# Attention and a depthwise convolution: a new order of work, and four steps moved to other engines

## The chip, the cores and the metric

The kernel runs on one core of one Trainium2 chip. It uses the core's engines side by side: TensorE (PE) for matrix products, VectorE (DVE), ScalarE (ACT) and GpSimd (POOL) for elementwise work, and SyncE (SP) for issuing transfers. POOL issues transfers too. Each engine takes its instructions from its own queue in order, and waits on semaphores for what other engines or transfers bring. The metric is the device time of one execution in microseconds (us); less is better. All data is float32.

## The reference

The input x has 16 images of 384 channels and 32 x 32 points. Two layers are computed, each with a group normalisation ahead (32 groups of 12 channels) and its input added behind:

```python
x = x + _L0_conv_ref(_gn(x), L0_conv_w_qkv, L0_conv_w_proj, L0_conv_b_proj)
x = x + _L1_conv_ref(_gn(x), L1_conv_weight)

# layer 0: attention over the 1024 points of an image, 8 heads of 48 channels
qkv = einsum('bnc,oc->bno', xt, w_qkv)
attn = softmax(einsum('bhnd,bhmd->bhnm', q, k) * SCALE)
out = einsum('bnc,oc->bno', einsum('bhnm,bhmd->bhnd', attn, v), w_proj) + b_proj

# layer 1: depthwise 7 x 7 convolution, padding 3, with a symmetrised weight
w_sym = (weight + rot90(weight, 1) + rot90(weight, 2) + rot90(weight, 3)) * 0.25
```

## The kernel before

**Tiles.** An image is three tiles of 128 channels by 1024 points. Heads go in pairs: four pairs per image, numbered `u` over the whole run (64 in all). `wqk` has its columns arranged so that three products give q and k of pairs 0 to 2 in full and one third of pair 3 each; `qk_rest` gathers pair 3 with six small transfers on POOL's queue.

**One image, or batch `b`.** `load_x` brings x to `xns[b]` on POOL's queue (one buffer: the next image can come only after the last use by `v_step`). `Stats.channels` takes per-channel statistics on DVE (`bn_stats`, L180). `exchange` (L184 to L195) spreads each group's twelve channels to all its rows by way of DRAM: three transfers on SP's queue. `groups` (L197 to L204) merges them on all 128 rows, three times 144 values, and raises the variance to the power -1/2 on POOL. `apply` (L206) normalises on DVE. Then come ten pieces on PE, called chunks: six `qk_step` (L216; 12 matmuls, copied out by ACT) and four `v_step` (L244; 12 matmuls, copied out by ACT).

**Attention.** A pair takes 16 steps (two halves of the queries, eight key tiles), so a batch takes 64 and the run 1024. `s_step` (L268) computes scores in PSUM (three buffers) and ACT takes the exponential to a tile `e`; `av_step` (L284) multiplies with v, which carries a column of ones, so the sums of the softmax come with it. `take` (L298) copies the result to `os_[u]`. `sums_out`, `invert` and `divide` (L304 to L334) send the sums through DRAM, take reciprocals on DVE, spread these over 64 rows each by way of DRAM, and multiply on DVE; for the last pair of a batch, six transfers on SP's queue put its rows to the other pairs.

**Projection and convolution.** `proj_step` (L338) computes a tile of the projection, and ACT adds the bias into a tile `y`. The old x was loaded again by `load_rest` (L138, POOL's queue), and `residual` (L352) adds `y` on DVE, giving x1. Statistics, exchange and merging follow as for x. `conv_begin` (L359) normalises x1 to `xn1s` on DVE, and 49 `conv_tap` (L363) on DVE each multiply a shifted window of it by one weight per channel and add it to x1 in place; `conv_end` (L375) stores the tile by POOL's queue. The very last tile is convolved on PE instead (`conv_on_pe` makes diagonal matrices on ACT, `conv_on_pe_run` multiplies, L380 to L415).

**The order.** The program is unrolled in Python by a planner (L497 to L698). It keeps two clocks, `clock` for PE and `vclock` for DVE, and adds fixed costs for each piece of work (L497). PE's part is a loop over groups of `GS` = 3 steps; in each turn the scores of a group are emitted and then the value steps of the group before, and where `credit` allows, one chunk of the next batch or one projection. `catch_up` (L526) then emits DVE's work until `vclock` has reached `clock`: first what is due in `later` (statistics, inversions and so on, entered by `after` with a delay and a cost), else a tap. Up to two tiles are open for taps, in turn. A batch's taps can start only when its x1 is there, so they are done during the next batch's attention. The framework beneath sets the semaphores, and puts the instructions of each engine in a queue; that order is near to the program's, and not always the same.

Of the kernel before, what the change touches and what calls it, by code (L numbers as in the profile page):

```python
# [16 lines left out]
P = 128  # L17
# [23 lines left out]
def kernel(  # L41
# [59 lines left out]
    def run(general):  # L101
        tag = "g" if general else "f"
        with ExitStack() as stack:
# [8 lines left out]
            epool = pool("epool", 5)  # L112
            opool = pool("opool", 5)
# [24 lines left out]
            def load_rest(b, k):  # L138

                x1s[b, k] = rpool.tile([P, N], F32, tag="x1", name=f"x1_{b}_{k}")  # L140
                nc.gpsimd.dma_start(
                    x1s[b, k], x[b, k * P : (k + 1) * P].rearrange("p h w -> p (h w)")
                )

# [13 lines left out]
            mhalf = wpool.tile([P, NK], F32, name="mhalf")  # L158
# [13 lines left out]

            class Stats:
# [10 lines left out]
                def exchange(self):  # L184
                    ch_d = ddram.tile([C, 12], F32, tag="ch", name=f"ch_{self.name}")
                    nc.sync.dma_start(ch_d.rearrange("(k p) s -> p k s", p=P), self.bs)
                    gr_d = ddram.tile([C, PER * 12], F32, tag="gr", name=f"gr_{self.name}")
                    nc.sync.dma_start(
                        gr_d.rearrange("(g e) s -> g e s", e=PER),
                        ch_d.rearrange("(g e) s -> g (e s)", e=PER)  # L190
                        .unsqueeze(1)
                        .to_broadcast([GROUPS, PER, PER * 12]),
                    )
                    self.gs = small.tile([P, NK, PER * 12], F32, tag="gs", name=f"gs_{self.name}")
                    nc.sync.dma_start(self.gs, gr_d.rearrange("(k p) s -> p k s", p=P))  # L195

                def groups(self):  # L197
                    self.mv = small.tile([P, NK, 2], F32, tag="mv", name=f"mv_{self.name}")
                    for k in range(NK):
                        nc.vector.bn_aggr(self.mv[:, k, :], self.gs[:, k, :])  # L200
                    ve = small.tile([P, NK], F32, tag="ve", name=f"ve_{self.name}")
                    nc.vector.tensor_scalar(ve, self.mv[:, :, 1], EPS, None, ALU.add)  # L202
                    self.rstd = small.tile([P, NK], F32, tag="rstd", name=f"rstd_{self.name}")
                    nc.gpsimd.tensor_tensor(self.rstd, ve, mhalf, ALU.pow)  # L204

                def apply(self, dst, src, k):  # L206
                    nc.vector.tensor_scalar(  # L207
                        dst,
                        src,
                        self.mv[:, k, 0:1],  # L210
                        self.rstd[:, k : k + 1],
                        ALU.subtract,
                        ALU.mult,
                    )
# [121 lines left out]
            ys = {}  # L336

            def proj_step(b, o):  # L338
# [10 lines left out]
                ys[b, o] = tpool.tile([P, N], F32, tag="t", name=f"y_{b}_{o}")  # L349
                nc.scalar.activation(halves(ys[b, o]), ps, AF.Identity, bias=bp[:, o : o + 1])  # L350

            def residual(b, o):  # L352
                nc.vector.tensor_tensor(x1s[b, o], x1s[b, o], ys.pop((b, o)), ALU.add)  # L353
# [25 lines left out]

            def conv_on_pe(b, k):  # L380

                DM = 2 * N // P
                diags = []
                for n, (dy, dx) in enumerate(TAPS):
                    if n % DM == 0:
                        dg = qkpool.tile([P, 2, N], F32, tag="qk", name=f"diag_{n}")
                        diags.append(flat(dg))
                    nc.scalar.mul(
                        diags[-1][:, n % DM * P : (n % DM + 1) * P],
                        ident,  # L390
                        wsym[:, k, dy + PAD, dx + PAD : dx + PAD + 1],
                    )
                return diags

            def conv_on_pe_run(b, k, diags):
                DM = 2 * N // P
# [58 lines left out]
            if general:  # L455
                for b in range(B):
# [5 lines left out]
                    st.exchange()  # L462
# [16 lines left out]
                    for o in range(NK):  # L479
                        load_rest(b, o)  # L480
                        proj_step(b, o)
                        residual(b, o)
                        st.channels(x1s[b, o], o)
                    st.exchange()
# [12 lines left out]
            US_STEP, US_TURN, US_QK, US_V, US_PROJ, US_TAP = 1.72, 0.35, 5.3, 4.0, 5.3, 1.02  # L497
# [3 lines left out]
            NS = U * 2 * NT  # L501

            def after(wait, cost, f):
                nonlocal count
                count += 1
                heapq.heappush(later, (clock + wait, count, cost, f))

            def tap():

                while len(active) < 2 and chains:  # L510
# [8 lines left out]
                c[2] += 1  # L519
                if c[2] < len(TAPS):  # L520
# [3 lines left out]
                return US_TAP  # L524

            def catch_up(to):  # L526
                nonlocal vclock
                while vclock < to:
                    if later and later[0][0] <= vclock:
                        _, _, cost, f = heapq.heappop(later)  # L530
                        f()
                        vclock += cost
# [8 lines left out]
            chunks = deque()  # L541
            ready = {}
            done = set()

            def issue(c):
                nonlocal clock
                kind, b, i = c
                done.add(c)
                if kind == "qk":
                    qk_step(b, *divmod(i, 2))  # L550
                    clock += US_QK
                    if i == 2 * NK - 1:
                        qk_rest(b)
# [193 lines left out]
```

## Time and profile before

| | |
|---|---|
| median of 3 runs | 3634.2 us (3633.62 to 3634.44) |
| the profiled execution | 3636.44 us |
| its span, first to last instruction | 3634.6 us |
| mean granted TensorE clock | 0.918 |
| taps on DVE (L366) | 2303, busy 2565.9 us |
| exponentials on ACT (L282) | 1024, busy 1012.2 us |
| scores on PE (L274) | 4096 matmuls, busy 973.7 us |
| values on PE (L290) | 4096 matmuls, busy 954.1 us |
| q and k on PE (L223) | 1152 matmuls, busy 531.1 us |
| residual on DVE (L353) | 48, busy 58.8 us |
| normalisation on DVE (L207) | 96, busy 73.6 us |
| merging of groups on DVE (L200) | 96, busy 68.1 us |

In the lines of the profile, times are in us unless marked ns. A group of instructions has its line, engine, operation, the tiles written and read with their shapes, a count, the busy time, the mean length of one in ns, and then the idle time of its engine just before and what ended it. Instructions of one engine overlap a little, so a sum of lengths is more than the busy time. A line of the list of waits reads: engine and line that waited, what it waited for, us in total, times, the longest. A line of the timeline has the start, the length, the engine, the line and the tiles, the count of merged instructions, and in brackets the idle time before it with its cause.

### The profile page before, as it was taken

The page shows a single profiled execution, that of the slowest core. Times are in us where ns is not written, and L with a number is a line of the kernel's source. Part 1 is how long each engine was busy: PE and PEld are TensorE (multiplying, and loading weights), DVE is VectorE, ACT ScalarE, POOL GpSimd, SP SyncE. Part 2 cuts the span into 40 slices and gives each one's busy share as a digit, 9 for nine tenths or more (in the row PEclk, how much of TensorE's full clock was granted, in tenths as well). Part 3 has the DMA queues.
Part 4 walks back from the last instruction along what each step waited for, and adds up shares of the span by engine and source line. Part 5 has one row for each costly group of instructions (what it writes and reads, how often), then busy time and mean ns, then how long its engine had stood idle before and what let it go on. Part 6 is the DMA issues. An engine that isn't in the chain of part 4 may idle for free.

```text
span 3634.6 us, 29118 instructions
## 1 busy us (share of the span) xinstructions
PE 3018.4 (83%) x10886; PEld 1140.3 (31%) x10886; DVE 2958.3 (81%) x2906; ACT 1297.8 (36%) x1474; POOL 173.6 (5%) x282
## 2 busy tenths in 40 slices
PE   7999979696996969789696986979699697979371
PEld 3333323232332323233232332323233232323130
DVE  1016969899696998969799796988989698797997
ACT  2444434242342424334242442434334243444100
POOL 1000000000000000000000000010000001000000
PEclk9999989898998989989898998989899798999686
DMA  3010110202111020211202111030111102011000
GB/s 115 13 48 18 56 39 18 77 12 66 33 56 38 19 65 24 61 33 37 58 17 65 29 56 39 13 83 18 61 33 56 38 7 83 23 37 36 28 11 19
DMA packets 96007, 148.68 MB, mean 41 GB/s; under 512 B 40272, under 2 KB 65632, under 8 KB 94320
## 3 DMA queue, kind: packets, MB, share of 16 engines
q0 software_dynamic: 23856, 88.17, 8.0%
q1 hardware_dynamic: 72000, 58.55, 6.6%
q8 instruction: 88, 1.44, 0.2%
q14 instruction: 63, 0.52, 0.0%
HBM read 101.00 MB, written 33.88 MB: 37 GB/s over the span
## 4 chain that ended last, share of the span: by engine, by line
DVE 66%; PE 19%; DMA 8%; issue 4%; POOL 1%; ACT 0%; SPq 0%; DVEq 0%; POOLq 0%
DVE x L366 58%; PE ps_proj L342 7%; PE ps_s L274 4%; PE acc L290 4%; PE ps_qk L223 3%; DMA inv<-inv 3%; DVE bs_x L180 2%; DVE mv_x L200 2%; DMA gr_x<-ch_x 1%; DVE o L326 1%; DMA gs_x<-gr_x 1%; DMA ch_x<-bs_x 1%; POOL rstd_x L204 1%; DMA inv<-rec 1%; DVE xn L207 1%
## 5 line engine op out<-in xcount | busy, mean ns | idle before, releaser
L366 DVE SCALAR_TENSOR_TENSOR x<-xn,wsym,x 128x930 f32<-128x930 f32 (+8 forms) x2303 | 2565.9, 1168 | 22.1
L282 ACT ACTIVATE e<-ps_s 128x1024 f32<-128x1024 f32 x1024 | 1012.2, 1022 | 534.4 <-PE acc L290 265.8
L274 PE MATMUL ps_s<-qk 48*128 48x512 f32 x4096 | 973.7, 607 | 0.0
L290 PE MATMUL acc<-e,v 128*64 128x512 f32 x4096 | 954.1, 601 | 0.0
L223 PE MATMUL ps_qk<-x,wqk 128*128 128x512 f32 x1152 | 531.1, 612 | 163.7 <-DVE x L207 163.7
L342 PE MATMUL ps_proj<-o,wp 128*128 128x512 f32 x576 | 281.5, 642 | 353.1 <-DMA o<-o 353.1
L274 PEld LDWEIGHTS ps_s<-qk 48*128 48x128 f32 x4096 | 366.4, 186 | 581.8 <-issue 414.4
L290 PEld LDWEIGHTS acc<-e,v 128*64 128x64 f32 x4096 | 263.7, 136 | 648.5 <-issue 648.3
L223 PEld LDWEIGHTS ps_qk<-x,wqk 128*128 128x128 f32 x1152 | 216.1, 194 | 476.3 <-issue 377.4
L230 ACT COPY qk<-ps_qk 128x1024 f32<-128x1024 f32 x96 | 97.2, 1012 | 709.1 <-PE ps_qk L223 709.1
L350 ACT ACTIVATE y<-ps_proj,bp 128x1024 f32<-128x1024 f32 x48 | 53.4, 1113 | 642.8 <-PE ps_proj L342 642.8
L342 PEld LDWEIGHTS ps_proj<-o,wp 128*128 128x128 f32 x576 | 114.0, 205 | 520.7 <-issue 488.2
L249 PE MATMUL ps_v<-wv,x 128*128 128x384 f32 x768 | 260.3, 492 | 0.0
L353 DVE TENSOR_TENSOR x<-x,y 128x1024 f32<-128x1024 f32 x48 | 58.8, 1224 | 197.5 <-ACT y L350 197.5
L180 DVE BATCH_NORM_STATS2 bs_x<-x 128x6 f32<-128x512 f32 x192 | 121.6, 680 | 81.8 <-DMA x<-in_x 80.5
L200 DVE BATCH_NORM_AGGREGATE mv_x<-gs_x 128x2 f32<-128x144 f32 x96 | 68.1, 765 | 145.0 <-DMA gs_x<-gr_x 145.0
L249 PEld LDWEIGHTS ps_v<-wv,x 128*128 128x128 f32 x768 | 142.1, 190 | 126.8 <-ACT e L282 21.9
L326 DVE TENSOR_TENSOR o<-o,inv 128x1024 f32<-128x1024 f32 x64 | 78.0, 1219 | 85.3 <-DMA inv<-inv 85.3
L258 ACT COPY v<-ps_v 128x384 f32<-128x384 f32 x128 | 55.1, 483 | 244.6 <-PE ps_v L249 244.6
L376 POOL DMA_DIRECT2D out<-x x48 | 27.3, 569 | 1842.3 <-DVE x L366 1808.5
L405 PE MATMUL ps_conv<-xn,diag 128*128 128x464 f32 (+8 forms) x196 | 77.7, 559 | 23.5 <-DVE xn L207 23.5
L204 POOL TENSOR_TENSOR rstd_x<-ve_x,mhalf 128x3 f32<-128x3 f32 x32 | 39.8, 1244 | 1072.7 <-DVE ve_x L202 1072.7
(33 smaller groups left out, 335.7 us busy)
## 6 DMA issues: line engine op xcount, KB each, us to landing
x<-in_x POOLq DMA_DIRECT2D x96, 512.0 KB, 5.6
inv<-inv SPq DMA_DIRECT2D x128, 256.0 KB
out<-x POOLq DMA_DIRECT2D x48, 512.0 KB, 2.9
qk<-qk POOLq DMA_DIRECT2D x96, 128.0 KB, 6.4
gr_x<-ch_x SPq DMA_DIRECT2D x32, 216.0 KB
gs_x<-gr_x SPq DMA_DIRECT2D x32, 216.0 KB
o<-o SPq DMA_DIRECT2D x96, 64.0 KB
sum<-o SPq DMA_DIRECT2D x128, 4.0 KB
```

Source lines behind the costliest of these rows:

```text
L180: nc.vector.bn_stats(self.bs[:, k, 6 * h : 6 * h + 6], src[:, h * HALF : (h + 1) * HALF])
L200: nc.vector.bn_aggr(self.mv[:, k, :], self.gs[:, k, :])
L223: nc.tensor.matmul(ps[:, h, :], lhsT=wqk[:, k, s, t, :], rhs=xns[b][:, k, h * HALF : (h + 1) * HALF], start=(k == 0), stop=(k == NK - 1),)
L230: nc.scalar.copy(halves(qks[u][:, s, :]), ps)
L249: nc.tensor.matmul(ps[:, j, 0:C], lhsT=xns[b][:, k, t * P : (t + 1) * P], rhs=wv[:, k, :], start=(k == 0), stop=(k == NK - 1),)
L274: nc.tensor.matmul(ps[:, j, :], lhsT=qks[u][r, 1, i * P : (i + 1) * P], rhs=qks[u][r, 0, h * HALF : (h + 1) * HALF], start=True, stop=True,)
L282: nc.scalar.activation(es[n], ps, AF.Exp, scale=SCALE)
L290: nc.tensor.matmul(accs[u, h][64 * j : 64 * j + 64, :], lhsT=v_of(u, i, j), rhs=e[:, j, :], start=(i == 0), stop=(i == NT - 1),)
L326: nc.vector.tensor_tensor(os_[u], os_[u], invs.pop(u), ALU.mult)
L342: nc.tensor.matmul(ps[:, h, :], lhsT=wp[:, t, o * P : (o + 1) * P], rhs=os_[NP * b + t][:, h * HALF : (h + 1) * HALF], start=(t == 0), sto ...
L366: nc.vector.scalar_tensor_tensor(acc, xn1s[b, k].rearrange("p (h w) -> p h w", w=W)[:, iy, ix], wsym[:, k, dy + PAD, dx + PAD : dx + PAD + 1],
L405: nc.tensor.matmul(ps[:, h, :].rearrange("p (y x) -> p y x", x=W)[:, lo - h * HH : hi - h * HH, ox], lhsT=diags[n // DM][:, n % DM * P : ( ...
```

## The change

- **Order.** The planner's costs are new (`us_tap` reckons a tap by its points, with a lower fixed part where another tile is open; delays of `after` count from the later of both clocks, and are longer). The group is four steps, and its value steps come in the same turn as its scores. Chunks are emitted when two credits are there, up to two in a turn; the three projections of a batch come in a row; `qk_rest` is a chunk of its own.
- **Taps.** Up to three tiles are open for taps, in turn.
- **Normalisation.** `apply` runs on ACT as scale times x plus bias.
- **Residual.** `load_rest`, `residual` and the tile `y` are gone. ACT writes the projection with its bias to the x1 tile, and a transfer on POOL's queue then adds x from DRAM to it.
- **Merging.** `gather` brings a group's twelve channels to one row each (32 rows); one merging on DVE, four small operations on POOL, and scale and bias go back to all channels by two transfers on SP's queue.
- **The last tile's convolution** is begun when its statistics are there, ahead of its batch's other tiles; its diagonals are made five per turn.
- `e` and `o` have six buffers instead of five.

```diff
-            epool = pool("epool", 5)
-            opool = pool("opool", 5)
+            epool = pool("epool", 6)
+            opool = pool("opool", 6)
...
-                def exchange(self):
+                def gather(self):
                     ch_d = ddram.tile([C, 12], F32, tag="ch", name=f"ch_{self.name}")
                     nc.sync.dma_start(ch_d.rearrange("(k p) s -> p k s", p=P), self.bs)
-                    gr_d = ddram.tile([C, PER * 12], F32, tag="gr", name=f"gr_{self.name}")
+                    self.gs = small.tile([GROUPS, PER * 12], F32, tag="gs", name=f"gs_{self.name}")
+                    nc.sync.dma_start(self.gs, ch_d.rearrange("(g e) s -> g (e s)", e=PER))
+
+                def groups(self):
+
+                    mv = small.tile([GROUPS, 2], F32, tag="mv", name=f"mv_{self.name}")
+                    nc.vector.bn_aggr(mv, self.gs)
+                    ve = small.tile([GROUPS, 1], F32, tag="ve", name=f"ve_{self.name}")
+                    nc.gpsimd.tensor_scalar(ve, mv[:, 1:2], EPS, None, ALU.add)
+                    af = small.tile([GROUPS, 2], F32, tag="af", name=f"af_{self.name}")
+                    nc.gpsimd.tensor_tensor(af[:, 0:1], ve, mhalf, ALU.pow)
+                    nc.gpsimd.tensor_tensor(af[:, 1:2], mv[:, 0:1], af[:, 0:1], ALU.mult)
+                    nc.gpsimd.tensor_scalar(af[:, 1:2], af[:, 1:2], -1.0, None, ALU.mult)
+                    gr_d = ddram.tile([GROUPS, PER, 2], F32, tag="gr", name=f"gr_{self.name}")
                     nc.sync.dma_start(
+                        gr_d, af.unsqueeze(1).to_broadcast([GROUPS, PER, 2])
                     )
+                    self.sc = small.tile([P, NK, 2], F32, tag="sc", name=f"sc_{self.name}")
+                    nc.sync.dma_start(
+                        self.sc, gr_d.rearrange("g e s -> (g e) s").rearrange("(k p) s -> p k s", p=P)
+                    )
 
                 def apply(self, dst, src, k):
-                    nc.vector.tensor_scalar(
+                    nc.scalar.activation(
                         dst,
                         src,
-                        self.mv[:, k, 0:1],
-                        self.rstd[:, k : k + 1],
-                        ALU.subtract,
-                        ALU.mult,
+                        AF.Identity,
+                        bias=self.sc[:, k, 1:2],
+                        scale=self.sc[:, k, 0:1],
                     )
...
-                ys[b, o] = tpool.tile([P, N], F32, tag="t", name=f"y_{b}_{o}")
-                nc.scalar.activation(halves(ys[b, o]), ps, AF.Identity, bias=bp[:, o : o + 1])
-
-            def residual(b, o):
-                nc.vector.tensor_tensor(x1s[b, o], x1s[b, o], ys.pop((b, o)), ALU.add)
+                x1s[b, o] = rpool.tile([P, N], F32, tag="x1", name=f"x1_{b}_{o}")
+                nc.scalar.activation(halves(x1s[b, o]), ps, AF.Identity, bias=bp[:, o : o + 1])
+                nc.gpsimd.dma_start(
+                    x1s[b, o],
+                    x[b, o * P : (o + 1) * P].rearrange("p h w -> p (h w)"),
+                    accum_op=ALU.add,
+                )
...
-            US_STEP, US_TURN, US_QK, US_V, US_PROJ, US_TAP = 1.72, 0.35, 5.3, 4.0, 5.3, 1.02
+            US_STEP, US_TURN, US_QK, US_V, US_PROJ = 1.716, 0.353, 5.3, 4.0, 5.3
...
+            GS = 4
...
+            def now():
+                return max(clock, vclock)
+
             def after(wait, cost, f):
...
-                heapq.heappush(later, (clock + wait, count, cost, f))
+                heapq.heappush(later, (now() + wait, count, cost, f))
+
+            def us_tap(dy, dx):
+                return ((H - abs(dy)) * (W - abs(dx)) + (130 if len(active) > 1 else 270)) / 960
 
             def tap():
 
-                while len(active) < 2 and chains:
+                while len(active) < NK and chains:
                     st, b, k = chains.popleft()
                     conv_begin(st, b, k)
...
+            def project(b):
+                nonlocal clock
+                for o in range(NK):
+                    proj_step(b, o)
                     clock += US_PROJ
-                    after(1.5, 1.3, lambda: x1_part(b, i))
+                    after(8.0, 1.3, lambda o=o: x1_part(b, o))
...
                 if k == NK - 1:
-                    st.exchange()
-                    after(max(0.0, vclock - clock) + 9.0, 2.5, lambda: x1_groups(b, st))
+                    st.gather()
+                    after(6.5, 0.8, lambda: x1_groups(b, st))
 
             def x1_groups(b, st):
                 st.groups()
+                after(9.0, 0.0, lambda: x1_chains(b, st))
+
+            def x1_chains(b, st):
+                if b == last[0]:
+                    conv_begin(st, *last)
+                    conv_on_pe(*last)
+                chains.extend((st, b, k) for k in range(NK) if (b, k) != last)
 
             def begin_x(b):
                 load_x(b)
-                after(9.0, 3.8, lambda: x_channels(b))
+                after(12.0, 3.8, lambda: x_channels(b))
...
+                after(9.0, 0.8, lambda: x_groups(b, st))
 
             def x_groups(b, st):
                 st.groups()
-                after(max(0.0, vclock - clock) + 1.5, 2.4, lambda: x_apply(b, st))
+                after(15.0, 0.0, lambda: x_apply(b, st))
...
-                ready[b] = max(vclock, clock) + 2.5
+                ready[b] = now() + 6.0
 
             def finish(u):
                 sums_out(u)
-                after(6.0, 0.3, lambda: finish2(u))
+                after(7.0, 0.3, lambda: finish2(u))
 
             def finish2(u):
                 invert(u)
-                after(max(0.0, vclock - clock) + 8.0, 1.3, lambda: finish3(u))
+                after(9.5, 1.3, lambda: finish3(u))
 
             def finish3(u):
                 b, p = divmod(u, NP)
                 divide(u)
                 if p == NP - 1:
+                    proj.append((now() + 4.0, b))
...
+            for n0 in range(0, NS, GS):
+                b, r = divmod(n0, PER_B)
+                if r == 0:
+                    while chunks:
+                        issue(chunks.popleft())
+                    if b + 1 < B:
+                        queue(b + 1)
+                for n in range(n0, n0 + GS):
                     s_step(n)
+                for n in range(n0, n0 + GS):
+                    av_step(n)
                     u, h, i = n // (2 * NT), n // NT % 2, n % NT
                     if i == NT - 1:
                         take(u, h)
                         if h == 1:
                             finish(u)
+                clock += GS * US_STEP + US_TURN
+
+                credit = min(credit + 12.0 * GS / PER_B, 2.0)
                 if proj and proj[0][0] <= clock:
+                    project(proj.popleft()[1])
+                elif credit >= 2:
+                    while chunks and credit >= 1:
+                        kind, cb, i = chunks[0]
+                        first = {"qk": 2 * NT * (i // 2), "v": 0, "rest": 2 * NT * 3}[kind]
+                        if ready.get(cb, 1e9) > clock or r + GS < first:
+                            break
                         issue(chunks.popleft())
                         credit -= 1
                 catch_up(clock)
+                if b == last[0] and r >= PER_B // 4:
+                    for n in range(len(TAPS)):
+                        if n // 5 == (r - PER_B // 4) // GS:
+                            diagonal(last[1], n)
```

## The prediction

> **What bounds the kernel now.** I read the engines' sums first, then the chain of waits, then the list of waits, then the two timelines of one batch.
>
> ```profile
> PE 3018.4 (83%) x10886; PEld 1140.3 (31%) x10886; DVE 2958.3 (81%) x2906; ACT 1297.8 (36%) x1474; POOL 173.6 (5%) x282
> DVE 66%; PE 19%; DMA 8%; issue 4%; POOL 1%; ACT 0%; SPq 0%; DVEq 0%; POOLq 0%
> PE ps_proj L342 <- DMA o<-o: 353.1, 11, 54.6
> PE ps_qk L223 <- DVE x L207: 163.7, 6, 28.1
> DVE x L353 <- ACT y L350: 197.5, 39, 9.6
> DVE mv_x L200 <- DMA gs_x<-gr_x: 145.0, 18, 11.8
> POOL out L376 <- DVE x L366: 1808.5, 42, 110.3
> ```
>
> No engine is full: PE is idle for 616 us, DVE for 676. The list of waits (us, times, longest) says why: PE waits for what DVE must finish first (o after the division, x after normalisation), DVE waits for what PE and the exchanges bring. They stand still in turn. The first two PE waits, 516.8 us, fall in 15 batches: 34 us each.
>
> The period comes from the chain of waits: batch 0's first taps start at 312.86, batch 14's at 3325.53, so p = 3012.7 / 14 = 215.2 us. Then 3634.6 = 312.9 + 14 p + 309.1. I predict these three terms.
>
> ```profile
> 1054.64 1.99 PE L274 MATMUL ps_s<-qk 48*128 48x512 f32 x8
> 1064.49 1.13 PE L274 MATMUL ps_s<-qk 48*128 48x512 f32 x4
> 1065.56 2.79 PE L290 MATMUL acc<-e,v 128*64 128x512 f32 x12
> 1123.95 8.23 PE L223 MATMUL ps_qk<-x,wqk 128*128 128x512 f32 x12 [28.09 <-DVE x L207]
> 1132.11 2.85 PE L274 MATMUL ps_s<-qk 48*128 48x512 f32 x12
> 1134.88 2.80 PE L290 MATMUL acc<-e,v 128*64 128x512 f32 x12
> 1137.61 5.42 PE L342 MATMUL ps_proj<-o,wp 128*128 128x512 f32 x12
> ```
>
> These are PE's rows: start, length, tile. One score step takes 1.07 us to the next row (1064.49 to 1065.56), two take 1.92, three 2.77: 0.85 each and 0.21 for the switch. Three value steps take 2.73, so a group of three steps is 5.50. PE now needs 21.33 x 5.50 + 6 x 5.35 (qk) + 4 x 4.07 (v) + 3 x 5.35 (proj) = 181.8 us a batch; 33.4 of 215.2 is idle.
>
> ```profile
> 1068.53 33.81 DVE L366 SCALAR_TENSOR_TENSOR x<-xn,wsym,x 128x841 f32<-128x841 f32 x28
> 1102.26 1.28 DVE L180 BATCH_NORM_STATS2 bs_x<-x 128x6 f32<-128x512 f32 x2
> 1130.88 7.01 DVE L366 SCALAR_TENSOR_TENSOR x<-xn,wsym,x 128x870 f32<-128x870 f32 x6
> 1144.21 1.23 DVE L353 TENSOR_TENSOR x<-x,y 128x1024 f32<-128x1024 f32 x1 [6.32 <-ACT y L350]
> 1155.06 1.22 DVE L353 TENSOR_TENSOR x<-x,y 128x1024 f32<-128x1024 f32 x1 [8.19 <-ACT y L350]
> 1176.11 2.13 DVE L200 BATCH_NORM_AGGREGATE mv_x<-gs_x 128x2 f32<-128x144 f32 x3 [7.66 <-DMA gs_x<-gr_x]
> 1218.57 45.61 DVE L366 SCALAR_TENSOR_TENSOR x<-xn,wsym,x 128x961 f32<-128x961 f32 x41
> ```
>
> DVE does 28 taps before the statistics of the next x, while PE waits (no PE row from 1095.8 to 1123.95). Once the old tiles are used up it starves on y and the exchange. The planner sets this order: it reckons 1.02 us a tap and 1.3 for residual and statistics together (2.5 here), so DVE is always late.
>
> **The change, part by part.**
>
> **Taps.** The 28 taps that follow one normalisation run on one tile: by the order of TAPS 25,864 elements, 26.94 us at 960 elements a us; 33.81 leaves 0.245 us a tap over. The 41 taps alternate between two tiles: 38,620 elements, 40.23 us, 0.131 over. Three in turn, which no row shows, I price as two; ends 0.10 and 0.245. A batch has 134,832 elements, 140.4 us, and 147 taps x 0.131: 159.7 us, against 2565.9 / 47 x 3 = 163.8 now: minus 4.1. A rule speaks against this: the Trainium skill, "VectorE: DVE Perf Modes", section "The DRAIN you can't avoid", says the next operation starts only when the pipe is empty, with or without semaphores between them. By it turns gain nothing, taps stay at 163.8, and DVE would need 178.7 a batch; with the wait for ACT below that is p = 184.5 and some 33 us more in the end. The two rows differ by 0.114 us a tap, and I follow them.
>
> **Off DVE.** From the groups, a sixteenth each: residual 58.8 (3.7), normalisation 37.5 + 36.1 (4.6), two of three aggregations 68.1 (2.8), ve 4.8 (0.3). Left per batch: 159.7 + statistics 7.6 + divisions 4.9 + reciprocals 1.0 + aggregation 1.4 = **174.6**, from 190.1.
>
> **On ACT.** Six normalisations at 1.11 (the row y<-ps_proj) add 6.7 to 81 us a batch: hidden beneath PE while ACT is under 180. But a tile's first tap now waits for an ACT instruction queued behind the exponentials of the group already issued. A group lasts 7.2 us and its last exponential ends about 5.2 in, so a start that falls early in it waits 6.3; with two qk steps behind the group (10.7) it waits up to 17, one that falls late 0. I take 5.8 of DVE idle per batch, near the plain group, as such steps follow only every third one. Behind the waiting tap stand all taps, reciprocals and divisions of DVE, and PE's next projection waits for those. Should ACT reach it before the scales land, every exponential behind it waits, and PE for those; the plan allows 9 and 15 us, and the two hops and small operations sum to about 7.
>
> **Residual.** The transfer replaces an addition, a y tile and the early loads (48 issues on POOL, 0.55 each, come and go). Plain loads of this size land in 4.0 us in the median, 8.1 at most (L141); accumulating has no row, and I take these two as its ends. From the projection's end: 1.2 for ACT, 0.6 issue, 4 to 8 landing: 5.8 to 9.8 against the 8.0 planned. DVE waits 0 to 3 us once per batch, as the later two parts come late by the same amount. It also stands in POOL's queue behind the stores, which wait for the last taps (1808.5 us): if DVE is late, so are these transfers, the next x load and the four small POOL operations.
>
> **Statistics.** An exchange of two wide hops on DRAM (216 KB each) becomes four small ones, two on each side of the aggregation; SP issues four instead of three. SP's queue now holds the scale transfers until POOL is done, with sums and inverses of pairs behind them: up to 7 us, once or twice a batch, within the 7.0 and 9.5 that the plan now gives those.
>
> **Groups of four.** The plan's own constants, 1.716 a step and 0.353 a group, give the 5.50 of the rows for three; 16 x (4 x 1.716 + 0.353) = 115.5 instead of 117.3: PE's floor is 115.5 + 32.1 + 16.3 + 16.1 = **179.9**. Each value step now comes in the iteration of its score step; four exponentials of 1.02 end 5.2 us in, while the fourth value step starts about 6.3 in, so no wait; that cover of 1.1 us is all there is. The sixth e and o buffers cost nothing; the 49 diagonals (0.39 each on ACT, 15.2 in all) are only spread out, and the last tile's convolution on PE (77.7) still lies beside 98 taps on DVE (106.5).
>
> **Sum.** PE's floor now stands above DVE's 174.6. What is late next is the projection: DVE is behind by 5.8 plus 0 to 3, say 7.2; the plan covers 0.9 of that (o lands 3.1 after the division of 3275.45 ends, the plan has 4.0) and the projection begins only at a group's end. With 6.3 us left over and a group's end 0 to 7.2 us off, the mean stall is 6.3 x 6.3 / 2 / 7.2 = 2.75. Ends: 0, and 17 + 3 less DVE's slack of 5.3 (179.9 - 174.6), less 0.9, less 3.6 (half a group): 10.2. So p = 182.65, ends 179.9 and 190.1. The head: three projections in a row save two groups (11 us), the longer way to the scales and ACT costs about as much: 313. The tail: 159.7 + 10.4 for batch 15's statistics, inverses and aggregation + 98 taps 106.5 + 1.2 + 18.6 (last tap to end, as now) = 296. Total 609 + 14 x 182.65 = **3166**. The profiled execution took 3636.4 with a span of 3634.6, the median is 3634.2: I add nothing.
>
> **Rivals.**
> *Half of the old trouble stays.* DVE runs on time in the plan, but the rows show that the queues aren't the program's order (L703, last in the code, runs at 3437 between taps): the order is re-made from estimates, and POOL's stores can still hold up loads. Against: most of the lateness came from tap and residual costs, now set right. With half of 33.4 idle: p = 179.9 + 16.7 = 196.6, total 3361.
> *Three in turn is no turn.* Each tap at 0.245 over: 176.5 + 14.9 + 5.8 = 197.2 a batch, and 28 more for the tail's 245 taps: total 3398. Against: the row of 41.
> *Slower: the accumulating transfer.* DVE's statistics wait in line for it, with all taps and divisions behind. From p = (3634.6 - 609) / 14 = 216.1 this loses: 41.5 us of DVE idle a batch, a landing some 50 us after the projection, twelve times a plain load. Nothing in the profile shows such a rate, nor rules it out, as the program has no accumulating transfer. With 48 us idle p is 222.6 and the total 3725.
>
> **How the numbers follow.** Forecast 0.63 (its own range 3128 to 3270, by the ends of p), half of the trouble 0.22, no turn 0.05, slower 0.10. About 0.2% is what a measurement of this kernel can tell from no change; from the second case I give 0.02 to that. So faster 0.88, same 0.02, slower 0.10. The range runs from 3110 (the low end less 18, a head or tail misjudged by that) to 3410, over both middle cases.
>
> **What would show it.** Right: PE busy above 93% in the middle, its waits for o and x under 5 us a batch, taps near 1.09 us, first taps 180 to 188 apart. Wrong: DVE waits above 10 us a batch for an accumulating transfer or for ACT, POOL stores holding x loads, or p near 197.

## The result, and the profile after

The changed kernel takes 3888.4 us in the median (3887.2 to 3890.9), against 3634.3 for the kernel before: 1.0698 of its time [1.0679, 1.0716]. It is slower, and lies far outside the range. The profiled execution has a span of 3885.2 us at a mean clock of 0.887, against 0.918 before.

The page's sums of the engines (busy us, share of the span, instructions) and its chain of waits, of the kernel after ("issue" is time in which the engine waited for nothing that the profile shows):

```profile
PE 3008.8 (77%) x10886; PEld 1165.3 (30%) x10886; DVE 2732.8 (70%) x2666; ACT 1371.3 (35%) x1570; POOL 195.1 (5%) x378
DVE 56%; PE 17%; issue 14%; DMA 8%; ACT 2%; POOL 2%; SPq 0%; ACTq 0%; POOLq 0%; DVEq 0%
```

DVE did get rid of work, from 2958.3 busy us to 2732.8, and PE's work is the same. Both are idle for longer: PE for 876 us of the span, 260 more than before. The prediction's three terms, read as it read them, from the first tap of batch 0 (302.96) to that of batch 14 (3577.02): 303.0 + 14 x 233.86 + 308.2 = 3885.2. The period was forecast at 182.65. The head (forecast 313) came 10 us lower and the tail (296) 12 higher; that the two nearly cancel is luck.

The list of waits of the kernel after (who waited for what: us in total, times, the longest) has a new first place among the engines on the path:

```profile
ACT x L204 <- DMA sc_x<-gr_x: 576.5, 15, 43.8
PE ps_s L270 <- ACT e L278: 552.0, 15, 43.2
DVE rec L311 <- DMA sums<-sum: 512.3, 18, 42.6
...
ACT xn L204 <- DMA sc_x<-gr_x: 188.3, 16, 29.0
PE acc L286 <- ACT e L278: 156.4, 15, 11.7
...
PE ps_proj L337 <- DMA o<-o: 56.7, 2, 51.5
```

PE's old waits, for o and for x, are nearly gone (56.7 for o, 353.1 before; 28.5 for x, 163.7 before). In their place ACT stands before the normalisation of x in 15 batches, up to 43.8 us each, and waits for the transfer of its scales. PE's wait for exponentials has the same count and nearly the same length: both engines stand still for one transfer of 3 KB. DVE works on meanwhile, and then waits in its turn for the sums of the softmax, which come from PE (29.7 us in the period that is shown last in this section). The same happens on a smaller scale before the normalisation of x1 (tile xn), with PE's wait at L286 behind it. One batch shows what is late. ACT's timeline of the kernel after (start, length, tile, idle time before it):

```profile
1630.19 3.77 ACT L278 ACTIVATE e<-ps_s 128x1024 f32<-128x1024 f32 x4 [3.44 <-PE ps_s L270]
1676.19 1.24 ACT L204 ACTIVATE x<-x,sc_x 128x1024 f32<-128x1024 f32 x1 [42.23 <-DMA sc_x<-gr_x]
...
1678.95 1.01 ACT L278 ACTIVATE e<-ps_s 128x1024 f32<-128x1024 f32 x1
```

The first normalisation stands in ACT's queue right behind the second group of four exponentials after the last `v_step`. The next exponential is behind it. PE's timeline of the same stretch:

```profile
1636.17 2.85 PE L270 MATMUL ps_s<-qk 48*128 48x512 f32 x12
1680.00 2.08 PE L270 MATMUL ps_s<-qk 48*128 48x512 f32 x4 [40.99 <-ACT e L278]
```

PE makes three more scores, until its three PSUM buffers are full, and stops for 41 us. What the scales wait for is in DVE's timeline, below POOL's row for the loads of that x:

```profile
1622.10 1.60 POOL L134 DMA_DIRECT2D x<-in_x  x3 [6.21 <-PE ps_v L245]
```

```profile
1651.97 8.33 DVE L363 SCALAR_TENSOR_TENSOR x<-xn,wsym,x 128x899 f32<-128x899 f32 x8
1660.22 3.64 DVE L174 BATCH_NORM_STATS2 bs_x<-x 128x6 f32<-128x512 f32 x6
1667.65 0.79 DVE L187 BATCH_NORM_AGGREGATE mv_x<-gs_x 32x2 f32<-32x144 f32 x1 [3.79 <-DMA gs_x<-ch_x]
```

The three loads of x were issued by 1623.7, and such a load landed in 4.6 us in the median and 10.9 at most in this run, so x was there by 1635 at the latest. Its statistics start at 1660.2, behind the last of the batch's 147 taps. From the end of their merging (1668.44) to ACT's start (1676.19) it is 7.8 us, so the transfers and small operations between them are not what is late. In the program the planner put the statistics among the taps, as the run with all queues held shows below; the framework, which puts the instructions into queues, placed them behind all taps, while it left ACT's normalisation early. The two queues no longer fit each other. By what the framework sorts, no run shows.

What this costs can be read from one period in the middle of the run (span, then busy us of PE, PEld, DVE, ACT and POOL):

```profile
1264.60:1500.40 235.80, 183.75 (x670) 70.61 (x668) 173.79 (x171) 84.83 (x96) 11.38 (x23) 0.88 0.14 35
```

PE is idle for 52 us of it. In this stretch PE waits for exponentials once for 41.1 us (L270), behind the normalisation of x, and once for 10.9 (L286), behind that of x1: together 52.0, all of its idle time.

### The profile page after: what moved, and what is told of

It is laid out like the page before. It is cut to its first block, busy times and chain, and to the rows that moved or that the text cites. A ratio compares the mean times of both kernels' runs of the same rounds, so it can differ in the third digit from the quotient of the medians.

```text
span 3885.2 us, 29202 instructions
## 1 busy us (share of the span) xinstructions
PE 3008.8 (77%) x10886; PEld 1165.3 (30%) x10886; DVE 2732.8 (70%) x2666; ACT 1371.3 (35%) x1570; POOL 195.1 (5%) x378
## 4 chain that ended last, share of the span: by engine, by line
DVE 56%; PE 17%; issue 14%; DMA 8%; ACT 2%; POOL 2%; SPq 0%; ACTq 0%; POOLq 0%; DVEq 0%
DVE x L363 54%; PE ps_proj L337 6%; PE acc L286 5%; PE ps_s L270 4%; DMA gr_x<-af_x 3%; DMA inv<-inv 2%; PE ps_qk L219 2%; DMA sc_x<-gr_x 2%; DVE o L322 1%; PE ps_v L245 1%; DMA inv<-rec 1%; ACT x L204 0%; POOL af_x L191 0%; ACT x L345 0%; ACT xn L204 0%
## 5 line engine op out<-in xcount | busy, mean ns | idle before, releaser
L363 DVE SCALAR_TENSOR_TENSOR x<-xn,wsym,x 128x930 f32<-128x930 f32 (+9 forms) x2303 | 2505.6, 1161 | 148.8 <-ACT xn L204 147.8
L270 PE MATMUL ps_s<-qk 48*128 48x512 f32 x4096 | 971.8, 613 | 552.0 <-ACT e L278 552.0
L278 ACT ACTIVATE e<-ps_s 128x1024 f32<-128x1024 f32 x1024 | 969.3, 1028 | 449.6 <-PE ps_s L270 445.5
L286 PE MATMUL acc<-e,v 128*64 128x512 f32 x4096 | 983.9, 623 | 156.4 <-ACT e L278 156.4
L270 PEld LDWEIGHTS ps_s<-qk 48*128 48x128 f32 x4096 | 377.8, 189 | 1131.9 <-ACT e L278 636.4
L219 PE MATMUL ps_qk<-x,wqk 128*128 128x512 f32 x1152 | 508.7, 598 | 28.5 <-ACT x L204 28.5
L286 PEld LDWEIGHTS acc<-e,v 128*64 128x64 f32 x4096 | 279.1, 141 | 829.0 <-issue 577.0
L337 PE MATMUL ps_proj<-o,wp 128*128 128x512 f32 x576 | 256.0, 604 | 56.7 <-DMA o<-o 56.7
L204 ACT ACTIVATE x<-x,sc_x 128x1024 f32<-128x1024 f32 x48 | 59.0, 1237 | 576.5 <-DMA sc_x<-gr_x 576.5
L297 ACT COPY o<-acc 128x512 f32<-128x512 f32 x128 | 74.8, 584 | 230.7 <-PE acc L286 230.7
L345 ACT ACTIVATE x<-ps_proj,bp 128x1024 f32<-128x1024 f32 x48 | 53.4, 1114 | 254.5 <-PE ps_proj L337 250.5
L235 POOL DMA_DIRECT2D qk<-qk x96 | 48.8, 512 | 1804.8 <-ACT e L278 1060.6
L204 ACT ACTIVATE xn<-x,sc_x 128x1024 f32<-128x1024 f32 x48 | 57.6, 1236 | 188.3 <-DMA sc_x<-gr_x 188.3
L187 DVE BATCH_NORM_AGGREGATE mv_x<-gs_x 32x2 f32<-32x144 f32 x32 | 25.4, 793 | 122.5 <-DMA gs_x<-ch_x 122.5
```

The lines of the kernel that those rows point to most:

```text
L204: nc.scalar.activation(dst, src, AF.Identity, bias=self.sc[:, k, 1:2], scale=self.sc[:, k, 0:1],)
L219: nc.tensor.matmul(ps[:, h, :], lhsT=wqk[:, k, s, t, :], rhs=xns[b][:, k, h * HALF : (h + 1) * HALF], start=(k == 0), stop=(k == NK - 1),)
L270: nc.tensor.matmul(ps[:, j, :], lhsT=qks[u][r, 1, i * P : (i + 1) * P], rhs=qks[u][r, 0, h * HALF : (h + 1) * HALF], start=True, stop=True,)
L278: nc.scalar.activation(es[n], ps, AF.Exp, scale=SCALE)
L286: nc.tensor.matmul(accs[u, h][64 * j : 64 * j + 64, :], lhsT=v_of(u, i, j), rhs=e[:, j, :], start=(i == 0), stop=(i == NT - 1),)
L297: nc.scalar.copy(os_[u][:, h * HALF : (h + 1) * HALF], accs.pop((u, h)))
```

## The experiments

The main theory, ORDER: the cost is in the queues' order, not in the work that was moved. The edit that tests it adds a dependency without a wait from each instruction of an engine to the one before it in the program, so that the queue has the planner's order. Only the list of engines differs between the runs that hold queues; some of them have further edits, which are named:

```diff
+        if not general:
+            pins = {'DVE'}
+            before = {}
+            for ins in list(nc.cur_bb.bb.instructions):
+                name = str(getattr(ins, "engine", "")).split(".")[-1]
+                if name in pins:
+                    if name in before:
+                        tc.add_manual_dep(ins, before[name], mybir.DependencyInfo(
+                            mybir.DependencyClass.NoSync, mybir.DependencyReason.DATA),
+                            reason="order")
+                    before[name] = ins.name
```

**The changed kernel, DVE's queue held** (`pins = {'DVE'}`).

> The changed kernel with DVE's queue held in the order in which the planner emits; the other queues are sorted by the framework as before. Theory ORDER (the queues are not in the planner's order: the statistics of the next x stand behind all 147 taps, so the scales come some 40 us late and ACT, and with it PE, waits): the wait of ACT's x normalisation for the scales falls from 576 us to under 150, the time to 3200 to 3400. Theory ACT (normalising x on ACT between the exponentials is what costs, wherever DVE's statistics stand): 3800 or more. Theory TRANSFER (the accumulating transfer and the four small hops are too slow): 3800 to 3900, DVE's waits for them stay.

Measured: 3679.6 us, 1.013 [1.0113, 1.0147]. The direction is ORDER's and 209 us come back, but the size missed: the time is 280 us above its range, and the wait, expected under 150 us, is 186.7. The list of waits of this run says why:

```profile
ACT xn L204 <- DMA sc_x<-gr_x: 440.7, 16, 32.8
...
ACT x L204 <- DMA sc_x<-gr_x: 186.7, 15, 14.2
```

The wait before x's normalisation fell from 576.5 to 186.7. That before the normalisation of x1 (tile xn) rose from 188.3 to 440.7: ACT's own queue is still re-sorted and asks for those scales too early; in the run below that holds ACT's queue too, this wait is 169.7.

**All five queues held** (`pins = {'DVE', 'PE', 'Activation', 'Pool', 'SP'}`).

> The changed kernel with the queues of all five engines held in the planner's order. ORDER: the plan now runs as written: 3130 to 3270, PE busy above 90%, ACT's waits for scales under 60 us in all. ACT: 3800 or more, as the x normalisation still stands between exponentials. TRANSFER: about 3850.

Measured: 3372.2 us, 0.9283 [0.9267, 0.9298]. The same work on the same engines is 516 us faster than as the framework sorts it. In DVE's timeline of this run x's statistics stand between taps, and ACT's row of the normalisation follows:

```profile
1353.45 29.07 DVE L363 SCALAR_TENSOR_TENSOR x<-xn,wsym,x 128x928 f32<-128x928 f32 x26
1382.45 3.65 DVE L174 BATCH_NORM_STATS2 bs_x<-x 128x6 f32<-128x512 f32 x6
...
1395.15 0.79 DVE L187 BATCH_NORM_AGGREGATE mv_x<-gs_x 32x2 f32<-32x144 f32 x1
```

```profile
1431.47 3.51 ACT L204 ACTIVATE x<-x,sc_x 128x1024 f32<-128x1024 f32 x3
```

ACT normalises 36 us after the merging, with no wait; in the whole run its wait there is 1.5 us. But 3372 is still 102 above the top of ORDER's number, PE is busy for 88% of the span and not above 90, and ACT's waits for the scales of x and x1 are 69.8 us (1.5 + 68.3), not under 60. So something else costs too.

**DVE and ACT held** (`pins = {'DVE', 'Activation'}`).

> The changed kernel with only DVE's and ACT's queues held in the planner's order. ORDER, in the form that these two queues carry the loss (the statistics' place on DVE and the normalisations' place on ACT): 3340 to 3450, near the 3372 of all five. If POOL's, SP's or PE's order matters as much: above 3500.

Measured: 3476.7 us, 0.956 [0.9544, 0.9576], between the two numbers. These two queues give 412 of the 516 us; PE's, POOL's and SP's, which were not held one by one, give the rest.

**x normalised on DVE again, queues as the framework sorts them.** In `x_apply`:

```diff
-                    st.apply(xns[b][:, k, :], xns[b][:, k, :], k)
+                    nc.vector.tensor_scalar(xns[b][:, k, :], xns[b][:, k, :],
+                        st.sc[:, k, 0:1], st.sc[:, k, 1:2], ALU.mult, ALU.add)
```

> The changed kernel with the normalisation of x (not of x1) back on DVE, as scale times x plus bias. ORDER: the statistics still come behind all taps, but ACT's exponentials no longer queue behind them; PE meets the late x only at its first q and k chunk, some 50 us later in its queue: 3300 to 3550. ACT: all of the loss is gone, 3130 to 3270. TRANSFER: 3800 or more.

Measured: 3567.9 us, 0.9822 [0.9806, 0.9839], 18 us above the range given. Three instructions a batch (1.24 us each on ACT, 0.81 on DVE), put back on DVE, take 320 us off: no exponential stands behind the scales of x any more. So their place in ACT's queue is what makes the late statistics expensive. The normalisation of x1 stays on ACT, and its wait for scales grows from 188.3 to 352.5 us.

**The kernel before, DVE's queue held.**

> The kernel before with DVE's queue held in its planner's order. ORDER: it suffers from re-sorting as well, but its plan reckons taps and residual too cheap, so DVE stays late: 3450 to 3640. ACT and TRANSFER say nothing of it: 3600 to 3670.

Measured: 3513.3 us, 0.9671 [0.9655, 0.9687]. The kernel before loses to the re-sorting as well, some 120 us on DVE's queue alone. With all of its queues held it was not tried.

**The kernel before, only x normalised on ACT.** In its `x_apply`, with the bias from one small operation on DVE:

```diff
+                nb = small.tile([P, NK], F32, tag="nb", name=f"nb_{b}")
+                nc.vector.scalar_tensor_tensor(nb, st.mv[:, :, 0], -1.0, st.rstd, ALU.mult, ALU.mult)
                 for k in range(NK):
-                    st.apply(xns[b][:, k, :], xns[b][:, k, :], k)
+                    nc.scalar.activation(xns[b][:, k, :], xns[b][:, k, :], AF.Identity,
+                        bias=nb[:, k : k + 1], scale=st.rstd[:, k : k + 1])
```

> The kernel before, queues sorted by the framework, with only the normalisation of x moved from DVE to ACT (the bias by one small DVE operation). ORDER: x's statistics stand behind taps here too, and ACT now waits for them with exponentials behind it, where PE waited only at its next q and k chunk: 3680 to 3900. Rival RELIEF (DVE is the bound and is relieved of 2.3 us a batch): 3560 to 3620.

Measured: 3770.4 us, 1.0376 [1.0357, 1.0396]. This one part alone makes the kernel before slower, although it takes work off DVE. The list of waits of this run has the two lines of the kernel after again, with the bias in the place of the scales:

```profile
ACT x L605 <- DVE nb L601: 547.3, 15, 42.7
PE ps_s L274 <- ACT e L282: 522.7, 22, 39.9
```

**x normalised on DVE with the queues held** (the kernel of the small operations, below, with the edit of the run on DVE and a cost of 2.3 in the plan).

> As the run with the small operations on DVE, in held order, and the normalisation of x (not of x1) back on DVE. ORDER (ACT is a harmful place only while the scales come late): within 40 us of that run, either way, as DVE has 2.3 us a batch more. ACT (the place between exponentials costs even in held order): at least 60 us less than that run.

Measured: 3329.2 us, 0.9151 [0.9136, 0.9167], against 3308.6 with x normalised on ACT. With x's scales in time, ACT is the better place, by 21 us.

**The accumulating transfer undone** (`load_rest`, the tile y and `residual` on DVE back in the changed kernel, with their delay and cost in the plan).

```diff
-                x1s[b, o] = rpool.tile([P, N], F32, tag="x1", name=f"x1_{b}_{o}")
-                nc.scalar.activation(halves(x1s[b, o]), ps, AF.Identity, bias=bp[:, o : o + 1])
-                nc.gpsimd.dma_start(x1s[b, o], ..., accum_op=ALU.add)
+                ys[b, o] = tpool.tile([P, N], F32, tag="t", name=f"y_{b}_{o}")
+                nc.scalar.activation(halves(ys[b, o]), ps, AF.Identity, bias=bp[:, o : o + 1])
...
```

> The changed kernel, queues sorted by the framework, with the early loads, the y tile and DVE's residual addition put back in place of the accumulating transfer. TRANSFER: the loss goes by 150 us or more, to 3740 or less. ORDER: the transfer (5.5 us to land in the changed kernel's trace, 4.0 for a load before) has no part in it: 3830 to 3950, DVE having 3.7 us a batch more to do.

Measured: 3864.2 us, 1.0624 [1.0606, 1.0642]. Only 24 us come back, so the transfer isn't the cause. ACT's wait for x's scales is 571.0 us there, nearly as in the kernel after.

**Six xn buffers instead of four, all queues held** (`npool = pool("npool", 6)`), to find the rest above the forecast.

> All five queues in the planner's order, and six buffers instead of four for the normalised x1 tiles. In the run with all five, ACT waited 114 us in 7 times for DVE's taps before it could write such a tile, with exponentials behind it. Theory SLOT: three open tiles need the next batch's three buffers beside their own, and this wait goes: 3250 to 3310. If it is only a lag of DVE that shows up there: 3350 to 3375.

Measured: 3369.5 us, 0.9274 [0.9249, 0.9299]. Nothing that can be told from 3372.2. The wait for a free xn tile (113.9 us in the list of the run with four buffers) is gone from the list, and the time stays: it was hidden behind something else. This theory fell.

**And the tail** (in addition, DVE's addition of the last tile's convolution entered 85 us later instead of at once).

```diff
-                    conv_on_pe(*last)
+                    ps = conv_on_pe(*last)
+                    after(85.0, 1.2, lambda: conv_on_pe_end(*last, ps))
```

> As the run with six buffers, and DVE's addition that ends the last tile's convolution on PE is emitted 85 us after the convolution begins instead of at once (in held order it kept the last batch's taps waiting 77 us): 60 to 80 us less than with six buffers alone, 3180 to 3250. This is the time that the forecast stood for, if its floor of PE holds.

Measured: 3349.3 us, 0.9205 [0.9189, 0.922]: 20 us less than with six buffers alone, where 60 to 80 were expected; the other figure of the expectation, 3180 to 3250, is lower than these 60 to 80 allow, and was missed as well. The timeline of the tail shows what took the gain, first POOL's row, then, from DVE's timeline, the row beside it:

```profile
3085.41 69.89 POOL L189 TENSOR_SCALAR ve_x<-mv_x 32x1 f32<-32x1 f32 x1 [14.08 <-DVE mv_x L187]
```

```profile
3085.25 69.96 DVE L363 SCALAR_TENSOR_TENSOR x<-xn,wsym,x 128x928 f32<-128x928 f32 x65
```

An addition on 32 numbers ran 69.89 us on POOL, as long as DVE ran taps without a pause. The last batch's normalisations of x1, and with them the last tile's convolution, waited for it: ACT stood for 95.03 us before them.

**The small operations on DVE, but for the power** (in `groups`, from the kernel above, all queues held).

```diff
-                    nc.gpsimd.tensor_scalar(ve, mv[:, 1:2], EPS, None, ALU.add)
+                    nc.vector.tensor_scalar(ve, mv[:, 1:2], EPS, None, ALU.add)
                     nc.gpsimd.tensor_tensor(af[:, 0:1], ve, mhalf, ALU.pow)
-                    nc.gpsimd.tensor_tensor(af[:, 1:2], mv[:, 0:1], af[:, 0:1], ALU.mult)
-                    nc.gpsimd.tensor_scalar(af[:, 1:2], af[:, 1:2], -1.0, None, ALU.mult)
+                    nc.vector.tensor_scalar(af[:, 1:2], mv[:, 0:1], af[:, 0:1], -1.0, ALU.mult, ALU.mult)
```

> As the run in held order with six buffers and the late addition (3349), and three of the four small operations of each merging go from POOL to DVE; the power stays on POOL with DVE waiting for it. Theory PORT (POOL's 32x1 operations, 0.2 us while DVE rests, take up to 70 us while DVE runs taps, and SP's scale transfers with sums and inverses behind them wait): these long rows go, DVE's waits for sums and inverses and PE's for o with them: 3230 to 3300. If the long rows are only POOL's own waiting shown as work: 3335 to 3360.

Measured: 3308.6 us, 0.9094 [0.9079, 0.9109], 41 less and 9 above the range. The long rows on POOL are gone, and the list of waits shows a new one: DVE waits 219.2 us, 32 times, for the power. In DVE's timeline of this run, with POOL's row of the power below:

```profile
1215.01 0.14 DVE L190 TENSOR_SCALAR ve_x<-mv_x 32x1 f32<-32x1 f32 x1
1232.40 0.20 DVE L192 TENSOR_SCALAR af_x<-mv_x,af_x 32x1 f32<-32x1 f32 x1 [17.25 <-POOL af_x L191]
```

```profile
1231.48 0.88 POOL L191 TENSOR_TENSOR af_x<-ve_x,mhalf 32x1 f32<-32x1 f32 x1
```

POOL did the power only at 1231.48, behind the three accumulating transfers of the projection, each of which waits for ACT.

**The same with POOL's queue left to the framework** (`pins = {'DVE', 'PE', 'Activation', 'SP'}`).

> As the run with the small operations on DVE (3309), but POOL's queue is left to the framework's sorting; the other four stay held. In that run DVE waits 17 us a batch for the power of x's statistics, which stands in POOL's queue behind three accumulating transfers that wait for ACT. Theory HEAD (this place in the queue is what is left of DVE's idle time): DVE's wait for the power falls from 219 us to under 60, the time to 3170 to 3270. If another wait takes its place: 3290 to 3330.

Measured: 3183.8 us (3180.3 to 3185.2), 0.8756 [0.8742, 0.8771]. It is faster than both kernels, by 12.4% than the one before. DVE's wait for the power fell from 219.2 us to 23.4, as HEAD said. So on POOL the planner's order was the bad one: it emits the power behind transfers that are not ready. What else moved in POOL's queue was not tried by itself. The engines' sums of this run, then, from its list of waits, the two that matter:

```profile
PE 2959.1 (93%) x10886; PEld 1155.9 (36%) x10886; DVE 2734.1 (86%) x2730; ACT 1370.0 (43%) x1570; POOL 167.4 (5%) x282
```

```profile
PE ps_s L271 <- ACT e L279: 32.7, 15, 3.7
...
DVE af_x L192 <- POOL af_x L191: 23.4, 32, 0.7
```

PE waits 32.7 us for exponentials in the run, instead of 552.0 + 156.4. The first taps are at 308.5 and, for batch 14, at 2875.60: 308.5 + 14 x 183.36 + 302.9 = 3178.5, where the forecast had 313 + 14 x 182.65 + 296.

## Why the prediction was wrong

**The step that failed** is the one on ACT: "Should ACT reach it before the scales land, every exponential behind it waits, and PE for those; the plan allows 9 and 15 us, and the two hops and small operations sum to about 7". The condition was named, and priced at nothing, because the time that the plan allows was taken for the time that the queues allow. The sum of about 7 was right where DVE ran no taps beside POOL (7.8 us in the batch shown). The runs showed that the queues follow the plan on neither side: DVE's statistics went behind all taps, ACT's normalisation stayed early, and ACT stood still for 576.5 us before x and 188.3 before x1, PE for exponentials for 552.0 + 156.4. In the period shown above that is 52.0 us of PE's time, all that it was idle, where the forecast had 2.75. Held in the planner's order, ACT's wait before x is 1.5 us and 516 us come back; in the kernel before, the move of x's normalisation alone costs 3.8%.

**The rival "Half of the old trouble stays"** named the cause: "the queues aren't the program's order". It was priced as a share of the old idle time, 33.4 us, so it could only come out faster. But an order that cost little for the old work, where x's normalisation waited on DVE among taps, costs much where it waits ahead of exponentials. Part of the evidence was in the trace of before: 28 taps stand ahead of x's statistics in the rows shown, and PE waited 28 us for x. With DVE's queue held, the kernel before has only 10 or 4 taps at that place (two batches of that run), so most of the 28 look like the work of the re-sorting. A price of 28 us a batch, worked out from that lateness on ACT's queue, would still have given 3166 + 14 x 28 = 3558, faster than before: with x normalised on ACT in the kernel before, ACT waited 547.3 / 15 = 36.5 us, and in the period of the kernel after PE lost 52.0. So the trace of before gave the place of the danger, and not its size.

**A second step was too small**: "the two hops and small operations sum to about 7" left out that POOL's four small operations run beside taps. That they stand behind transfers the prediction said, and gave it no time. In the kernel after neither shows, as DVE runs no taps just then (median 220 ns at L189). Once the queues were held both did: the change under its own order takes 3372.2 us, 206 above the forecast. Of these, 23 came back with the six buffers and the later addition, 41 with three of the four operations moved off POOL, and 125 with POOL's queue left to the framework, which let the power past the transfers.

**Point by point.**
- Taps, three in turn: 2505.6 / 2303 = 1.088 us each, 159.9 a batch; predicted 159.7. The turn of three is worth what the turn of two was (0.133 us a tap over the elements, against 0.131 in the row of 41). The rival "Three in turn is no turn" fell, and so did the reading by which turns gain nothing: the section that the prediction cites, "The DRAIN you can't avoid", itself says that a next operation that is not held starts earlier, which the prediction left out.
- DVE 174.6 a batch: a period of 235.8 us in the middle of the run has 173.8 busy.
- PE's floor 179.9: a group takes 7.2 us in its rows, three projections 15.66 (reckoned: 16.1). PE's 183.75 busy us in the period shown are near it, but 52.0 of waiting come on top; in the best version the period is 183.4.
- "first tap waits for ACT", 5.8 us: 147.8 / 16 = 9.2, within the ends of 0 and 17. One normalisation took 1.24 us, not 1.11.
- The accumulating transfer, 4.0 to 8.1: it landed in 5.1 to 8.0, 5.5 in the median. "Slower: the accumulating transfer" had the right sign of the outcome with the wrong cause: undone, it gives 24 us.
- The stall of 2.75 from DVE's lateness: 183.4 - 179.9 = 3.5 in the best version, near it in size; that this rest is the stall that was meant isn't shown.

So the terms for PE's and DVE's work held, and the forecast failed first by believing that the queues follow the plan. The plan's order alone doesn't give the forecast either: it takes 3372.2 us. The 3183.8 of the best version, 18 us from the forecast, needed POOL's queue out of the plan's order and three operations off POOL. That it is so near is in part luck.

## What to carry to other kernels

Before an instruction is moved onto an engine that feeds the bottleneck, look up in the trace where it will stand in that engine's queue and when its inputs come in this trace, not in the plan; a late input costs the engine's whole queue, and so it is priced with all that stands behind it. Where a framework re-sorts queues, a plan written out by hand is a wish: compare the rows' order with the program's first, and hold it by dependencies without waits where they differ. Hold only the queues where the plan is better, as here POOL's was not.

## What the hardware showed

The length of a GpSimd operation beside DVE was not expected. The same 32x1 addition took 0.22 us in the median in the kernel after, where 31 of the 32 have no tap beside them (the other, beside six taps, took 6.04). In the run with the later addition it took 2.9 in the median and 69.89 at most. There, 22 of the 23 rows that are longer than 0.3 us end within 0.2 us of the end of a run of taps. One of them, with DVE's row:

```profile
1255.04 7.23 POOL L189 TENSOR_SCALAR ve_x<-mv_x 32x1 f32<-32x1 f32 x1 [23.12 <-DVE mv_x L187]
```

```profile
1254.89 7.31 DVE L363 SCALAR_TENSOR_TENSOR x<-xn,wsym,x 128x841 f32<-128x841 f32 x7
```

The Trainium skill, "SBUF — State Buffer", section "Who interferes with whom", says that a DVE instruction with two inputs from SBUF contends with a GpSimd instruction that reads SBUF; the page's "Summary: rules for kernel authors" has it that the later of the two blocks until the first is done. A tap has two such inputs, and the rows agree with the contention, but not with one instruction's length: 65 taps of 1.08 us passed before POOL got through. That POOL's reads are what is held up was not tried by itself.

An accumulating transfer of 512 KB landed in 5.5 us in the median (kernel after), where the early plain load took 4.0 (kernel before, L141) and the load of x 4.6 (kernel after, L134); its issue took 0.88 us in the median on POOL against 0.54.
